# A state-space scan and a window-attention block on one core: the first image's convolution phase reordered, and the planner's PSUM banks written into the program

## The chip, the core and the metric

One core of one Trainium2 chip runs the whole program. Its engines are named as the profile names them: PE (matrix products; PEld is its weight load), DVE (vector), ACT (activation), POOL and SP (which here only issues DMAs). The metric is device microseconds (us) of one execution. Before the change three executions gave 7610.15, 7621.01 and 7637.82 us, a median of 7621.01 us.

## What is computed

The input is 8 images of 192 channels of 64x64 points, float32. Two layers follow each other. Per image:

```python
# layer 0: state-space scan
x = W_in @ x                                  # 192 -> 384 channels
x = depthwise_conv3x3(x) + b_dw               # 'SAME'
p = W_xd @ x                                  # 384 -> 16
Gl, Gm, Gr, L, U, D = (W @ p for W in ...)    # for 4 directions x 384 channels
Gl, Gm, Gr = each / (|Gl| + |Gm| + |Gr| + 1e-7)
for step in range(8):                         # chunks of 8 columns
    h = L * xs + Gl * up(h) + Gm * h + Gr * down(h)
    y += w_m[d] * (h * U + xs * D)            # 4 directions d: x, x^T, both flipped
y = grn(layernorm(y));  x = W_out @ y         # 384 -> 192
# layer 1: 8x8 windows, 6 heads, top-16 scores per row kept
s = layernorm(x); q, k, v = W_qkv @ s
x2 = s + proj(softmax(top16(normed(q) . normed(k)) + bias) @ v)
out = x2 + fc2(gelu(fc1(layernorm(x2))))
```

## The kernel before, in words

**Two parts.** A first phase, written out by hand, loads the constants and does the projection and the convolution of image 0 alone. All the rest comes from a planner: a `Plan` object collects steps (engine, cost, function, what is read and written), simulates them in `run` (L175) and hands them out in one order, in which they are then recorded (L1688 ff.). The steps are: `scan` of image b, the `front` (projection and convolution) of image b+1 and the `windows` of image b-1, side by side.

**The first phase** (L329 to L501). `load` (L334) alternates between two DMA queues, that of SP and that of ACT, so half of the constants are issued from ACT's own stream, ahead of ACT's first work. Image 0 comes in four strips of 16 rows (`xa`, `xb`, L367 and L370). There are 12 units: 3 channel tiles `ct` by 4 strips `u`. For each unit, `projected` (L432) has PE multiply by `w_in` into a PSUM tile `pin` (L439, L442) and ACT copy it into the bordered image `full` (L443). Nine units are convolved on DVE (`convolved`, L462: nine instructions over a strip, L468 and L470) and three, those of `ct` 2 with `u` 1 to 3, on PE (`convolved_by_products`, L473: nine products per half strip with a diagonal matrix `dg` that ACT makes at L487; ACT copies the sum out at L483). `stored` (L445) has ACT lay each unit out twice (`sn` L450, `st` L454), and SP writes both to DRAM (L451, L457). The order in the stream is: project unit n, convolve unit n-1 and store it; so ACT's copy of unit n+1 stands behind its stores of unit n-1. The convolution of a strip reads one row of the next strip.

**The folding** (L503 to L576). Biases and scales are folded into weights: `w_cv` from `w_dw`, `w_g2` times `w_m`, the mean taken out of `w_out`, three bias rows with small products on PE (`bias_row`, L527), `w_f1` times its norm's scale. It works in pools of its own, `prep` and `prep_ps`, which open after the pools of the convolution are closed and take over their memory, so the first instruction waits until the last store of the convolution has landed. Its loads (L506, L531, L542) are issued by SP at that place. The folded bias rows are written into their weights by a DMA from SP (L544).

**The start of the scan.** `x0`, the first chunk of image 0 (L762), goes into memory that the first phase used; then a product (L769), a copy (L779), a way through DRAM (L784, L792) and the gate products (L809) lead to the first DVE instruction of the scan (L842).

**PSUM banks.** From the scan on, six of the eight banks belong to the pool `l_ps`, all under one tag, "lp"; tiles are called `lp` or `g` (the scan's). The planner models the six banks as slots and gives a new tile the slot whose last user ended first in its simulation (L285). The recorded program does not know that slot: the tile pool gives the bank that was released first, in the order of the recorded instructions, by the last reader in that order. A tile's first product waits until the previous tile of its bank has been read for the last time; PE takes its instructions in the recorded order, so everything behind waits too.

Of the kernel before, what the change touches and what calls it, by code (L numbers as in the profile page):

```python
# [23 lines left out]
F32 = mybir.dt.float32  # L24
U8 = mybir.dt.uint8
AF = mybir.ActivationFunctionType
ALU = mybir.AluOpType
AX = mybir.AxisListType
PSUM = bass.MemoryType.PSUM
DRAM = bass.MemoryType.DRAM  # L30

P = 128
B, DM, H, W = 8, 192, 64, 64
DIN, ND, NS = 384, 4, 16
CT = DIN // P
CH = 8
HEADS, HD, WS = 6, 32, 8
HALF = DM // 2
# [6 lines left out]
RG = 32  # L45
# [9 lines left out]
class Held:  # L55


    def __init__(self, pool, shape, name, bufs=None, tag=None, dtype=F32):
        self.args = pool, shape, dtype, name, tag or name, bufs or pool.bufs
        self.tag, self.bufs = (id(pool), tag or name), bufs or pool.bufs  # L60
        self.users, self.left, self.end, self.next, self.tile = [], 0, 0.0, None, None

    def make(self):
        if self.tile is not None:
            return
        pool, shape, dtype, name, tag, bufs = self.args
        self.tile = pool.tile(shape, dtype, name=name, tag=tag, bufs=bufs)

    def __call__(self):
# [10 lines left out]
class Plan:  # L80
# [67 lines left out]
    def order(self):  # L148

        before = [s.before for s in self.steps]
        tiles = {h: h.left for s in self.steps for h in s.held}
        best = None
        for n in range(self.RUNS):
            for s, k in zip(self.steps, before):
                s.before, s.ready = k, 0.0  # L160
            for h, k in tiles.items():
                h.left, h.end, h.next = k, 0.0, None
            run = self.run()
            if best is None or self.length < best[0]:
                best = self.length, run, [s.start for s in run]
            for s in run:
                needs = [d.start for d in s.after] + [h.next.start for h in s.held if h.next]
                rank = min(needs, default=s.end) - (s.end - s.start)
                s.rank = (s.rank + rank) / 2 if n else rank
        self.length, run, starts = best  # L170
        for s, t in zip(run, starts):
            s.start = t
        return run

    def run(self):  # L175

        slots, queues = {}, {}
        counted, full = {}, {}
        done = []
# [16 lines left out]
        for s in self.steps:  # L196
            for h in s.makes:
                queues.setdefault((h.tag, s.lane), []).append(s)
                slots.setdefault(h.tag, [(0.0, k, None) for k in range(h.bufs)])
        first = {k: 0 for k in queues}  # L200

        def kept(tag):
# [58 lines left out]
        while todo:  # L261
            for e in dirty_plain:
                best_plain[e] = picked(e, None, plain[e], ready)
            for e in dirty | dirty_plain:
                best[e] = picked(e, best_plain[e], makers[e], room)
            dirty_plain, dirty = set(), set()
            e = min((x for x in engines if best[x]), key=lambda x: best[x][1])
            _, t, s = best[e]
            s.start = t
            if e == "PE":  # L270
                lead, cycles, share = s.cost
                end = stream(t + lead, cycles, share)
                free[e], s.end = end, end + 140.0
            else:
                hold, more = s.cost
                free[e] = t + hold
                s.end = free[e] + more
            (makers if s.makes else plain)[e].remove(s)
            dirty_plain.add(e)
            todo -= 1  # L280
            done.append(s)
            for tag in needs.get(s, ()):
                first[tag, s.lane] += needs[s][tag]
            for h in s.makes:
                slot = min(slots[h.tag], key=lambda x: x[:2])  # L285
                slots[h.tag].remove(slot)
                if slot[2]:
                    slot[2].next = s
            touched = bool(s.makes)
            for h in s.held:  # L290
                h.left -= 1
                h.end = max(h.end, s.end)
                if not h.left:
                    slots[h.tag].append((h.end + self.HOP, h.users[0].n + h.bufs, h))
                    touched = True
            for d in s.after:
                d.before -= 1
                d.ready = max(d.ready, s.end + (self.HOP if d.engine != e else 30.0))
                if not d.before:
                    wake(d)  # L300
                    if not d.makes:
                        dirty_plain.add(d.engine)
                    elif d.lane:
                        dirty.add(d.engine)
                    else:
                        touched = True
            if touched:
                dirty.update(engines)
# [10 lines left out]
def tile_ss2d_then_window_attention(ctx: ExitStack, tc: tile.TileContext, a: dict, out: bass.AP):  # L319
# [6 lines left out]
    nc = tc.nc  # L326
# [1 line left out]

    const = ctx.enter_context(tc.tile_pool(name="const", bufs=1))  # L329

    queues = [nc.sync, nc.scalar]
    n_loads = 0

    def load(name, src=None, rows=None):  # L334

        nonlocal n_loads
        src = a[name] if src is None else src
        shape = list(src.shape)
        t = const.tile([rows or shape[0]] + shape[1:], F32, tag=name, name=name)
        if rows:  # L340
            nc.gpsimd.memset(t[HALF:rows], 0.0)
        queues[n_loads % 2].dma_start(t[0 : shape[0]], src)
        n_loads += 1
        return t

    def blank(name, shape, value=None, engine=nc.gpsimd):
# [12 lines left out]
    ident = blank("ident", [P, P])  # L359
    make_identity(nc, ident)  # L360

    w_in = load("w_in")
    w_dv = load("w_dv")
    xa = epool.tile([P, H, W], F32, name="xa")
    xb = epool.tile([P, NG // 2, 8, W], F32, name="xb")
    for u in range(NG // 2):
        nc.sync.dma_start(xa[:, 16 * u : 16 * u + 16, :], x[0, 0:P, 16 * u : 16 * u + 16, :])  # L367
        for k in range(2):
            row = 16 * u + 8 * k
            nc.scalar.dma_start(xb[64 * k : 64 * k + 64, u], x[0, P:DM, row : row + 8, :])  # L370
        if u == 0:
            vecs = load("vecs")
    full = [epool.tile([P, H + 2, W + 2], F32, name=f"full{ct}") for ct in range(CT)]
    for t in full:
        nc.vector.memset(t[:, 0 : H + 2 : H + 1, :], 0.0)
# [50 lines left out]
        h.make()  # L426
    with early, tc.tile_pool(name="early_ps", bufs=2, space=PSUM) as early_ps:

        taps = [(dy, dx) for dy in range(3) for dx in range(3)]
        dg = epool.tile([P, 9, P], F32, name="dg")  # L430

# [30 lines left out]
        def convolved(ct, u):  # L462

            acc = epool.tile([P, 16, W], F32, name="acc", bufs=3)
            for n, tap in enumerate(taps):
                w = w_dv[:, ct, n : n + 1]
                if n == 0:
                    nc.vector.tensor_scalar(acc, near(ct, u, *tap), w, b_dw[:, ct : ct + 1], ALU.mult, ALU.add)  # L468
                else:
                    nc.vector.scalar_tensor_tensor(acc, near(ct, u, *tap), w, acc, ALU.mult, ALU.add)  # L470
            stored(ct, u, acc)

        def convolved_by_products(ct, u):  # L473

            acc = epool.tile([P, 16, W], F32, name="acc", bufs=3)
            for k in range(2):
                pc = early_ps.tile([P, CH, W], F32, name="pc")
                for n, (dy, dx) in enumerate(taps):
# [4 lines left out]
                nc.scalar.activation(acc[:, 8 * k : 8 * k + 8, :], pc, AF.Identity, bias=b_dw[:, ct : ct + 1])  # L483
            stored(ct, u, acc)

        for n in range(9):
            nc.scalar.activation(dg[:, n, :], ident, AF.Copy, scale=w_dv[:, CT - 1, n : n + 1])  # L487
        units = [(ct, u) for ct in range(CT) for u in range(NG // 2)]
        by_vector = [(ct, u) for ct, u in units if ct < CT - 1 or u == 0]
        by_tensor = [c for c in units if c not in by_vector]  # L490
        done = 0
        for ct, u in units:
            projected(ct, u)
            while done < len(by_vector) and by_vector[done] < (ct, u):
                convolved(*by_vector[done])
                done += 1
            while by_tensor and by_tensor[0] < (ct, u):
                convolved_by_products(*by_tensor.pop(0))
        for c in by_tensor:
            convolved_by_products(*c)  # L500
        assert done == len(by_vector)  # L501

    with tc.tile_pool(name="prep", bufs=2) as prep, tc.tile_pool(name="prep_ps", bufs=2, space=PSUM) as prep_ps:  # L503

        w_dw = prep.tile([3 * RG, CT * 4 * 3], F32, name="w_dw")
        nc.sync.dma_start(w_dw, a["w_dw"])  # L506
        id3 = prep.tile([3 * RG, RG], F32, name="id3")
        nc.vector.tensor_add(id3, ident[0 : 3 * RG, 0:RG], ident[0 : 3 * RG, RG : 2 * RG])
        nc.vector.tensor_add(id3, id3, ident[0 : 3 * RG, 2 * RG : 3 * RG])
# [17 lines left out]
        def bias_row(name, dst, products, *more):  # L527

            n = dst.shape[-1]
            row = prep.tile([1, n], F32, name="row_" + name)  # L530
            nc.sync.dma_start(row, a[name])  # L531
            for at in range(0, n, 384):
                m = min(384, n - at)
                ps = prep_ps.tile([P, 512], F32, name="ps_pre")
# [3 lines left out]
                    )  # L538
                nc.vector.tensor_add(row[:, at : at + m], row[:, at : at + m], ps[0:1, 0:m])
            for extra in more:  # L540
                got = prep.tile([1, n], F32, name="more_" + name)
                nc.sync.dma_start(got, a[extra])  # L542
                nc.vector.tensor_add(row, row, got)
            nc.sync.dma_start(dst[HALF : HALF + 1, 1, :], row)  # L544


        bias_row("b_qk", w_qk, [(n1_b[:, ci : ci + 1], w_qk[0:HALF, ci, :]) for ci in range(2)])
# [1225 lines left out]
```

## Time and profile before

| what | us |
|---|---|
| three runs, median | 7621.01 |
| the profiled execution, its own time | 7623.82 |
| its span, first to last instruction | 7622.0 |
| PE busy (share of the span) | 6699.8 (88%) |
| DVE busy | 6364.3 (83%) |
| POOL busy | 6229.7 (82%) |
| ACT busy | 4896.1 (64%) |
| mean granted PE clock (share of full) | 0.860 |

Busy time is per engine and overlaps. Idle time stands in the rows in front of the instruction that ended it, with the releaser: who set the semaphore it waited for last. In a timeline a row merges like instructions: start, busy us, engine, line, operation, how many; in square brackets the idle time before. ACTq and SPq are the parts of ACT and SP that issue DMAs. The end of a matrix product is modelled in the trace, so PE's busy time is not PE at its peak.

### The profile page before, as it was taken

What the parts mean: (1) busy time and instruction counts of PE and PEld (TensorE: products, weight loads), DVE (VectorE), ACT (ScalarE), POOL (GpSimd) and SP (SyncE); (2) the same over time, 40 slices, a digit from 0 to 9 for tenths busy, and PEclk for the clock granted to TensorE, in tenths of its full rate; (3) what the DMA queues carried; (4) which work ended last, traced back from release to release, by engine and by line L of the source; (5) the groups of instructions that cost most, each with busy time, mean ns of one, the idle gap of its engine ahead of it and who ended that gap; (6) DMA issues with size and microseconds to landing.
All of it is one profiled execution on the core that took longest, in us unless ns stands there. A gap on an engine that the chain in (4) does not pass through costs nothing. (4 is left out here: it accounts for less than half of the span.)

```text
span 7622.0 us, 141764 instructions
## 1 busy us (share of the span) xinstructions
PE 6699.8 (88%) x50180; PEld 3458.4 (45%) x50180; DVE 6364.3 (83%) x15477; ACT 4896.1 (64%) x9649; POOL 6229.7 (82%) x6333
## 2 busy tenths in 40 slices
PE   5888789988998899888999899988888888888987
PEld 2333344444444444444444444444444444444554
DVE  5687788998899988988888988889899989889643
ACT  2455456765776657675777757766576756666665
POOL 0688888998899988988888888889899989899422
PEclk7888789987988889898998889988888878888999
DMA  3666455312551245312551135411211111111100
GB/s 107 164 174 163 121 139 135 101 51 75 154 145 46 55 134 151 89 46 78 157 139 47 50 105 143 124 50 46 60 50 50 49 59 52 49 45 45 32 22 14
DMA packets 988331, 669.39 MB, mean 88 GB/s; under 512 B 651972, under 2 KB 814215, under 8 KB 987623
## 3 DMA queue, kind: packets, MB, share of 16 engines
q1 hardware_dynamic: 985638, 656.86, 32.1%
q8 instruction: 398, 6.52, 0.4%
q10 hardware_dynamic: 1984, 3.48, 0.2%
q14 instruction: 311, 2.54, 0.1%
HBM read 433.98 MB, written 226.18 MB: 87 GB/s over the span
## 5 line engine op out<-in xcount | busy, mean ns | idle before, releaser
L809 PE MATMUL g<-xe,w_g 32*128 32x512 f32 x3648 | 1171.5, 749 | 224.4 <-DVE dx L968 74.6
L809 PE MATMUL g<-xo,w_g 32*128 32x512 f32 x3648 | 1189.1, 729 | 184.5 <-DVE dx L968 90.9
L866 ACT ACTIVATE ab<-g 128x512 f32<-128x512 f32 x1344 | 784.6, 596 | 393.0 <-PE nb L809 168.9
L897 POOL TENSOR_TENSOR ab<-ab 128x512 f32<-128x512 f32 x672 | 865.0, 1287 | 162.7 <-ACT ab L866 151.0
L929 POOL TENSOR_TENSOR pw<-pw,rr 128x512 f32<-128x512 f32 x672 | 867.4, 1291 | 135.6 <-ACT rr L912 115.4
L914 POOL TENSOR_TENSOR pw<-pw,pq 128x512 f32<-128x512 f32 x672 | 881.0, 1311 | 82.5 <-DVE pq L873 53.2
L918 POOL TENSOR_TENSOR pw<-pw,pq 128x512 f32<-128x512 f32 x672 | 878.1, 1307 | 15.5
L982 POOL TENSOR_TENSOR dx<-dx,hu 128x512 f32<-128x512 f32 x576 | 742.9, 1298 | 112.1 <-DVE hu L973 97.1
L910 ACT ACTIVATE rr<-nb,eps 128x512 f32<-128x512 f32 x672 | 462.0, 687 | 571.7 <-DVE nb L907 569.1
L809 PEld LDWEIGHTS g<-xo,w_g 32*128 32x128 f32 x3648 | 410.5, 208 | 719.3 <-DVE dx L968 192.9
L809 PEld LDWEIGHTS g<-xe,w_g 32*128 32x128 f32 x3648 | 408.9, 212 | 704.8 <-DVE dx L968 173.1
L1628 PE MATMUL lp<-hd,w_f 128*64 128x256 f32 (+1 forms) x2304 | 594.9, 497 | 56.1 <-ACT hd L1614 15.0
L990 POOL TENSOR_TENSOR y<-y,dx 128x512 f32<-128x512 f32 x384 | 597.6, 1563 | 2.2
L696 PE MATMUL lp<-strip,w_cv 128*32 128x256 f32 x8064 | 563.5, 418 | 27.6 <-DMA strip<-pad 19.2
L925 DVE SCALAR_TENSOR_TENSOR nb<-nb,rr 128x512 f32<-128x512 f32 x672 | 464.8, 692 | 142.5 <-ACT rr L912 140.3
L934 DVE SCALAR_TENSOR_TENSOR nb<-nb,pw 128x512 f32<-128x512 f32 x672 | 464.7, 692 | 138.4 <-POOL pw L929 136.2
L907 DVE TENSOR_TENSOR nb<-nb,ab 128x512 f32<-128x512 f32 x672 | 465.3, 692 | 113.1 <-POOL ab L897 103.5
L973 DVE TENSOR_TENSOR hu<-g,hid 128x512 f32<-128x512 f32 x768 | 518.7, 681 | 1.0 <-PE g L809 0.7
L809 PE MATMUL nb<-xe,w_g 32*128 32x512 f32 x672 | 479.1, 800 | 12.5 <-DVE hid L942 12.3
L888 ACT ACTIVATE nb<-nb 128x512 f32<-128x512 f32 x672 | 399.5, 594 | 137.7 <-DVE pq L875 78.2
L980 POOL TENSOR_TENSOR y<-hu,dx 128x512 f32<-128x512 f32 x192 | 246.3, 1289 | 291.7 <-DVE hu L973 289.7
L809 PE MATMUL nb<-xo,w_g 32*128 32x512 f32 x672 | 463.1, 774 | 14.6 <-DVE hid L942 14.6
(221 smaller groups left out, 16684.8 us busy)
## 6 DMA issues: line engine op xcount, KB each, us to landing
strip<-pad SPq DMA_DIRECT2D x1008, 132.0 KB
xd<-xsT SPq DMA_DIRECT2D x384, 256.0 KB
x<-xs SPq DMA_DIRECT2D x64, 768.0 KB
xd<-xs SPq DMA_DIRECT2D x192, 256.0 KB
z<-y SPq DMA_DIRECT2D x64, 768.0 KB
zg<-z SPq DMA_DIRECT2D x64, 768.0 KB
pad<-xin SPq DMA_DIRECT2D x168, 264.0 KB
xsT<-sn SPq DMA_DIRECT2D x168, 256.0 KB
```

Of the source, the lines that this page charges most:

```text
L696: nc.tensor.matmul(pc()[q * RG : (q + 1) * RG, k * 256 : (k + 1) * 256].rearrange("p (h w) -> p h w", h=4), lhsT=w_cv[:, ct, q, dx, :], rh ...
L809: nc.tensor.matmul(dst, lhsT=w[rows, col : col + P], rhs=xp[rows, :], start=True, stop=True)
L866: lambda r=r: nc.scalar.activation(ab()[:, r, :], g[r](), AF.Abs),
L897: plan("POOL", gp(512), lambda: nc.gpsimd.tensor_add(ab()[:, 0, :], ab()[:, 0, :], ab()[:, 1, :]), w=[ab])
L907: plan("DVE", vec(512), lambda: nc.vector.tensor_add(nb(), nb(), ab()[:, 0, :]), r=[ab], w=[nb])
L914: plan("POOL", gp(512), lambda: nc.gpsimd.tensor_add(one(), one(), pq()[:, 0, :]), r=[(pq, 0)], w=[pw])
L918: lambda: nc.gpsimd.tensor_add(one(), one(), pq()[:, 1, :]),
L929: plan("POOL", gp(512), lambda: nc.gpsimd.tensor_mul(one(), one(), rr()), r=[rr], w=[pw])
L973: lambda: nc.vector.tensor_mul(like(hu(), d), like(pu(), d), state(d, ct)),
L982: plan("POOL", gp(512), lambda: nc.gpsimd.tensor_add(dx(), dx(), hu()), r=[hu], w=[dx])
L990: nc.gpsimd.tensor_add(y, y, dx().rearrange("p (c i) -> p i c", c=CH))
L1628: nc.tensor.matmul(dst[:, at : at + rhs.shape[-1]], lhsT=lhsT, rhs=rhs, **flags)
```

## The change

Two independent things.

**First phase.** All constants but `w_in`, `w_dv` and `vecs` are issued by SP. All 12 units are projected first, in one run; `dg` is made after the fourth. Then the nine DVE units follow in order, each with its store, and after the fifth, seventh and eighth of them one unit by products each, whose `acc_p` has two buffers of its own. The `prep` pool is opened together with the convolution's pools instead of behind them, its loads are issued before the convolution, and the folding uses the convolution's PSUM pool. The folded bias rows are written into the weights from ACT's queue instead of SP's.

**Banks.** The planner remembers the number of the slot that it gave each tile, and keeps those of its best run. When a tile under "lp" is made, it asks for the tag of its slot, "lp0" to "lp5", with one buffer each: so it gets the planned bank.

```diff
 class Held:
+        self.slot = 0
     def make(self):
         pool, shape, dtype, name, tag, bufs = self.args
+        if tag == "lp":
+            tag, bufs = f"{tag}{self.slot}", 1
         self.tile = pool.tile(shape, dtype, name=name, tag=tag, bufs=bufs)
...
-                best = self.length, run, [s.start for s in run]
+                best = self.length, run, [s.start for s in run], {h: h.slot for h in tiles}
...
-        self.length, run, starts = best
+        self.length, run, starts, slots = best
+        for h, k in slots.items():
+            h.slot = k
...
                 slot = min(slots[h.tag], key=lambda x: x[:2])
                 slots[h.tag].remove(slot)
+                h.slot = slot[3]
...
-    queues = [nc.sync, nc.scalar]
-    def load(name, src=None, rows=None):
+    def load(name, src=None, rows=None, queue=nc.sync):
...
-        queues[n_loads % 2].dma_start(t[0 : shape[0]], src)
-        n_loads += 1
+        queue.dma_start(t[0 : shape[0]], src)
...
-    w_in = load("w_in")
-    w_dv = load("w_dv")
+    w_in = load("w_in", queue=nc.scalar)
+    w_dv = load("w_dv", queue=nc.scalar)
...
-            vecs = load("vecs")
+            vecs = load("vecs", queue=nc.scalar)
...
+        prep = early.enter_context(tc.tile_pool(name="prep", bufs=1))
+        w_dw = prep.tile([3 * RG, CT * 4 * 3], F32, name="w_dw")
+        nc.sync.dma_start(w_dw, a["w_dw"])
+        added = {}
+        for name in ("b_qk", "b_pr", "n1_br"):
+            added[name] = prep.tile([1, a[name].shape[-1]], F32, name="row_" + name)
+            nc.sync.dma_start(added[name], a[name])
...
-            acc = epool.tile([P, 16, W], F32, name="acc", bufs=3)
+            acc = epool.tile([P, 16, W], F32, name="acc_p", bufs=2)
...
-        for n in range(9):
-            nc.scalar.activation(dg[:, n, :], ident, AF.Copy, scale=w_dv[:, CT - 1, n : n + 1])
...
-        for ct, u in units:
+        for n, (ct, u) in enumerate(units):
             projected(ct, u)
-            while done < len(by_vector) and by_vector[done] < (ct, u):
-                convolved(*by_vector[done])
-                done += 1
-            while by_tensor and by_tensor[0] < (ct, u):
-                convolved_by_products(*by_tensor.pop(0))
-        for c in by_tensor:
-            convolved_by_products(*c)
+            if n == 3:
+                for m in range(9):
+                    nc.scalar.activation(dg[:, m, :], ident, AF.Copy, scale=w_dv[:, CT - 1, m : m + 1])
+        for n, c in enumerate(by_vector):
+            acc = convolved(*c)
+            stored(*c, acc)
+            if n in (4, 6, 7):
+                convolved_by_products(CT - 1, (4, 6, 7).index(n) + 1)
 
-    with tc.tile_pool(name="prep", bufs=2) as prep, tc.tile_pool(name="prep_ps", bufs=2, space=PSUM) as prep_ps:
-
-        w_dw = prep.tile([3 * RG, CT * 4 * 3], F32, name="w_dw")
-        nc.sync.dma_start(w_dw, a["w_dw"])
+        prep_ps = early_ps
...
-            nc.sync.dma_start(dst[HALF : HALF + 1, 1, :], row)
+            nc.scalar.dma_start(dst[HALF : HALF + 1, 1, :], row)
```

## The prediction

> **What bounds the kernel now.** I read four views: the slices, the table of engines by stage, the timeline of the first 230 us, and the waits of PE. The slices first:
>
> ```profile
> PE   5888789988998899888999899988888888888987
> DVE  5687788998899988988888988889899989889643
> POOL 0688888998899988988888888889899989899422
> ```
>
> From the third slice (190 us each) to the last three, PE, DVE and POOL are all at eight or nine tenths: no engine is the bound alone, and a stall of one is soon a stall of the others. The first slice is another regime: POOL at zero, PE and DVE half busy. Only there can much be won by order. The timeline of DVE (start, busy us, engine, line, operation, count, idle before) shows its skeleton:
>
> ```profile
> 27.42 0.81 DVE L468 TENSOR_SCALAR acc<-full,w_dv,vecs 128x1024 f32<-128x1024 f32 x1 [25.28 <-ACT full L443]
> ...
> 118.99 10.60 DVE L470 SCALAR_TENSOR_TENSOR acc<-full,w_dv,acc 128x1024 f32<-128x1024 f32 x8
> 181.33 0.19 DVE L508 TENSOR_TENSOR id<-ident 96x32 f32<-96x32 f32 x1 [51.74 <-DMA xs<-st]
> ...
> 183.10 1.35 DVE L510 TENSOR_TENSOR w_cv<-id,w_dw 96x1152 f32<-96x1152 f32 x1 [1.36 <-DMA w_dw<-in_w_dw_dram]
> ...
> 200.09 0.36 DVE L576 TENSOR_TENSOR rpb<-rpb,top_b 128x192 f32<-128x192 f32 x1
> 223.14 0.69 DVE L842 TENSOR_TENSOR hid<-g,x 128x512 f32<-128x512 f32 x1 [22.70 <-PE g L809]
> ```
>
> Nine convolved units run from 27.42 to 129.6 without a gap (11.35 each); then DVE stands still for 51.74 us, because the three units by products run after it on PE (products 122.15 to 174.0) and the folding's memory is free only when the last store has landed; then the folding, 181.33 to 200.45; then 22.70 us until the scan. SP issues the load of `x0` at 200.47, at the end of DVE's last folding instruction. So the whole phase is one chain, and all three big engines wait for its end. Why it starts late is in ACT's rows:
>
> ```profile
> 19.68 2.75 ACTq L342 DMA_DIRECT2D w_f<-in_w_f_dram  x2
> 22.46 1.28 ACT L487 ACT_TABLE_LOAD   x1 [22.46 <-DMA temp<-in_temp_dram]
> 23.75 2.74 ACT L487 ACTIVATE dg<-ident,w_dv 128x128 f32<-128x128 f32 x9
> 26.39 1.91 ACT L443 COPY full<-pin 128x1024 f32<-128x1024 f32 x2
> ```
>
> PE had the first `pin` at 11.62 (10.28 + 1.34, L442); ACT copied it at 26.39, behind its DMA issues, its table and `dg`.
>
> **The first phase, step by step.** The times are those of the new order, made of rows of the old one.
>
> 1. *Start.* ACT now issues 11 DMAs ahead of its first work: eight `xb` (7.63), `w_dv` (0.41) and two that SP issued before at 0.40 and 0.43. From 0.71 that is until 9.6; with the table (1.28) 10.9. `pin` is there at 11.6, the copy takes 1.05: DVE begins at about 12.8 instead of 27.42. `dg` (2.74) goes behind the fourth copy, where PE has a second `pin` to fill. The loads go to SP, whose stream ended at 27.76: eleven more there, 12 us by ACT's rows without `xb`'s, make 40, and SP's next work, the first store, is due near 48. Loads later than that would cost nothing until the stores' three buffers are full.
>
> 2. *Nine units on DVE.* 9 x 11.35 = 102.2, as before, if `acc` is free. It has three buffers, and ACT now copies all 12 projections before it stores the first unit. Unit 4 begins at 12.8 + 3 x 11.35 = 46.9 if unit 1 has been stored. PE's later units in each burst take 1.98 + 1.13 = 3.11 (rows at 32.23 and 34.15): 11.6 + 11 x 3.11 = 45.8 for the last product, +1.05 copy, +1.05 and +1.98 for the first store = 49.8. So DVE stalls 2.9 and ends at 12.8 + 102.2 + 2.9 = 117.9. This is where the new order is nearest to a loss; the clock decides:
>
> ```profile
> 40.00:60.00 20.00, 10.93 (x16) 3.36 (x16) 19.36 (x16) 6.47 (x7) 0.00 (x0) 0.62 0.38 105
> 140.00:160.00 20.00, 20.00 (x49) 8.53 (x48) 0.00 (x0) 6.48 (x8) 0.00 (x0) 1.00 0.19 52
> ```
>
> (busy PE, PEld, DVE, ACT, POOL; then the granted clock.) In the old order PE works in bursts and gets 0.62; busy throughout it gets 1.00. At 27.44, after 12.8 idle, four products take 3.78, a few us later 1.98. The new projections are one run, so I take the fast row. The Trainium skill ("TensorE: Matmul & The Clock Gate", Part 1: The HAM clock gate) says it as a rule: half speed by default, full after some 3.4 us of sustained work, and half again after an idle window. Against it, the same page warns that the gate was seen stuck low; by that the sum would be the cold rival's below.
>
> 3. *Three units by products.* 15.5 each warm (31.17 for two). The first two half strips can run from 46; the rest follow as ACT frees `pc` behind the stores of units 5, 7 and 8: the last is summed near 115, copied and laid out (2 x 0.69 + 1.05 + 1.98) by 119.5. The last DVE unit is stored by 122, issued by SP at 122; before, the last issue at 177.70 let DVE go at 181.33, 3.6 later, so 126. All of it lies beside DVE; the cover is the folding, to 135, 9 us.
>
> 4. *Folding.* 181.33 to 200.45 = 19.1 before. Two waits for its loads go (1.36, and 0.52 for `more_b_pr`): 17.2. The 51.74 go wholly: no memory is waited for. What is late next is the folding's own chain, PE and DVE in turn (13.51 and 4.95 of mutual waits are in the 17.2). 117.9 + 17.2 = 135.1. The two bias stores (0.65, 0.53) move to ACT's stream, idle until PE's first planned product behind the folding; without that cover 1.2. SP loses them ahead of `xt`; `x0` waits for the folding, not for SP.
>
> 5. *Onward.* `x0` at 135.1 instead of 200.47: **65 us**. The 22.7 to the scan are the same instructions. Behind it, the recorded order of every engine is the same as before, instruction for instruction, so the rest moves as a block, but for the banks.
>
> **The banks.** I followed each of the 6360 tiles of the six banks through the instruction records, with its predecessor in the bank by each program's order. 5428 keep theirs, 932 get another. In the old trace 580 tiles wait for their bank, 539 us of PE's 910 idle; but only 74 of these are among the 932, with 69 us. Put the new predecessor's end, in the same trace, in place of the old: 37.8 us of PE's idle go (67 tiles), 11.2 come (42 tiles, held back where they were not). The commonest wait of PE (us in total, times, longest), and the clearest single case:
>
> ```profile
> PE g L809 <- DVE dx L968: 165.5, 110, 7.1
> ```
>
> ```profile
> 3905.30 1.05 PE L1453 MATMUL lp<-ident,at 128*128 128x128 f32 x4 [4.27 <-DVE hu L973]
> ```
>
> The first is a bank wait: `dx` and `hu` are the last readers of a `g`. In the second, PE stands 4.27 us for a `hu` while the bank of the new plan had been free 3.6 us earlier. Net 26.6 on PE. How much of it reaches the end no row says: all of it if PE never waits for another engine, nothing if it always would have. PE is the busiest at 88%, with DVE and POOL at 83 and 82, so I take half, **13**; the ends kept are 38 gained and 11 lost.
>
> **Sum.** 7623.8 (profiled execution, 1.8 around the span, 2.8 over the median) - 65 - 13 = **7546**. The first phase may be 58 to 68 (stall 0 to 10), the banks +11 to -38: 7518 to 7577. 0.3%, about 23 us, is what a measurement can tell from no change.
>
> **Rivals.**
>
> *Cold projections.* If PE gets the clock of the old bursts: 3.78 + 1.3 a unit, last product at 6.6 + 12 x 5.1 = 67.8, first store done at 71.9 instead of 49.8. DVE stalls 25 instead of 2.9, the phase gains 43: **7568**. For it: 0.62 in the row of the old phase. Against: 1.00 where PE is busy throughout. 0.10.
>
> *The planned banks let out a cascade.* Each wait that goes brings the next products closer to the plan, and others of the 539 us, on tiles whose bank is the same, shrink too. A tenth of them beyond the forecast is 54: **7492**. For it: the engines are locked together. Against: these waits have the same predecessor. 0.07.
>
> *The phase's gain is spent in the scan of image 0.* The slices show that second stage at eight tenths, and `strip` loads there wait for DMA; if the front, not `x0`, led it, SP's stream would still start it, from 122 instead of 194, so little could be lost. Half of 65: **7578**. 0.04.
>
> *Slower: the planned banks are freed later than planned.* 462 of the 932 tiles get a predecessor that ended later in the old trace, by 315 us together. The planner's ends are a model's; the old order asked only who was read first. All 315 on PE: 7624 - 65 + 315 = 7874. It decides from 65 + 23 = 88, more than a quarter of the 315; the trace shows 11.2, 4%, the rest being covered by products in front. **7700**, say, at 45%. 0.03.
>
> *It doesn't do what it says.* The recorded orders show that it does: ACT's copies ahead of the stores, 932 other banks. Only the effect could be nil, if ACT were held by something else to 26: then step 1 is lost (14.6) and the stall too: **7558**, inside the range. 0.02, with the forecast at 0.74.
>
> **How the numbers follow.** Forecast 7518 to 7577 with 0.74. To leave out no more than 0.2 with the uncertain share of the banks, the range goes up over the cold case and part way to the cascade: **7505 to 7595**. Faster by over 0.3%: 0.74 + 0.10 + 0.07 + 0.04 + 0.02, less 0.03 for milder ends of the slower case that eat up the gain: 0.94. Within: 0.03. Slower: 0.03.
>
> **What would show it.** Step 1: DVE's first L477 near 12.8. Step 2: no idle over 10 us between the units, PE's projections in one run at 3.1 each. Step 4: no wait for a store ahead of the folding; `x0` issued near 135, the scan's first DVE instruction near 158. Banks: PE's idle, 910 us, down by about 90: 65 of the first phase's, the rest from bank waits; the row of `dx` at L809 smaller. I am wrong if the first scan instruction comes after 175, or if it comes at 158 and the span is still not near 7545: then the banks, or the block that I moved unchanged, are it.

## The result and the profile after

The changed kernel takes **7548.4 us** (median of four runs, 7541.67 to 7558.15); the kernel before, four runs beside it, 7626.0 (7610.15 to 7637.82). The ratio is 0.9896, 95% interval [0.9878, 0.9913]. The forecast was 7546 in a range of 7505 to 7595. The profiled execution took 7551.0 us, its span is 7549.2 (before 7622.0).

The slices of the changed kernel, now 189 us each:

```profile
PE   7888799898989899888999899989888888898887
DVE  6787798988899889898898988889899988899543
POOL 1898788998899989987988888889899989899422
```

Only the first slice is another one: PE seven tenths instead of five, POOL already begins in it. From the second on, the rows look as they did. The timeline of DVE (start, busy, engine, line, operation, count, idle before) has a new skeleton:

```profile
14.64 0.83 DVE L477 TENSOR_SCALAR acc<-full,w_dv,vecs 128x1024 f32<-128x1024 f32 x1 [12.50 <-DMA xb<-in_x_dram]
...
48.74 0.81 DVE L477 TENSOR_SCALAR acc<-full,w_dv,vecs 128x1024 f32<-128x1024 f32 x1
...
106.02 10.53 DVE L479 SCALAR_TENSOR_TENSOR acc<-full,w_dv,acc 128x1024 f32<-128x1024 f32 x8
116.47 0.18 DVE L510 TENSOR_TENSOR id<-ident 96x32 f32<-96x32 f32 x1
...
132.45 0.16 DVE L568 TENSOR_TENSOR b_f<-b_f,ps_pre 128x6 f32<-128x6 f32 x1 [5.44 <-PE ps_pre L565]
...
133.96 0.36 DVE L575 TENSOR_TENSOR rpb<-rpb,top_b 128x192 f32<-128x192 f32 x1
153.72 0.69 DVE L841 TENSOR_TENSOR hid<-g,x 128x512 f32<-128x512 f32 x1 [19.40 <-PE g L808]
```

The first unit begins at 14.64 (before 27.42). The fourth, 48.74, has no idle before it. The folding begins as the ninth unit ends, 116.47, where 51.74 us of waiting stood. The scan starts at 153.72 instead of 223.14: **69.4 us earlier**. The same DVE instructions later run 65.9 us earlier around 300 us, 73.3 around 3000, 65.9 around 5000, and 72.8 at the end. So the first phase brings nearly all of it.

PE in the same execution: the twelve projections end at 44.65, then the products of the three units, then the folding's and the front's.

```profile
44.65 15.72 PE L489 MATMUL pc<-full,dg 128*128 128x512 f32 x36
74.93 17.19 PE L489 MATMUL pc<-full,dg 128*128 128x512 f32 x36 [14.56 <-ACT acc_p L492]
97.47 17.87 PE L489 MATMUL pc<-full,dg 128*128 128x512 f32 x36 [5.35 <-ACT acc_p L492]
...
126.18 6.23 PE L565 MATMUL ps_pre<-n_gb,w_f 128*128 128x1 f32 x24
132.71 3.56 PE L649 MATMUL lp<-xt,w_in 128*128 128x512 f32 x4 [0.30 <-issue]
136.21 1.13 PE L652 MATMUL lp<-xt,w_in 64*128 64x512 f32 x4
137.27 0.86 PE L768 MATMUL lp<-x,w_xd 128*32 128x128 f32 x24
```

And SP's issues:

```profile
121.70 0.36 SPq L466 DMA_DIRECT2D xs<-st  x1
...
126.66 0.59 SPq L761 DMA_DIRECT2D x<-xs  x1
```

`x0` (L761) is issued at 126.66, 8 us ahead of the folding's end. Its product (L768) still starts only at 137.27: PE takes it behind L565, L649 and L652. The scan now waits for PE's queue, not for `x0`.

PE's commonest wait, which was to shrink:

```profile
PE g L808 <- DVE dx L967: 176.1, 110, 7.1
```

The wait of `g` for `dx` is 176.1 us, where it was 165.5.

### The profile page after: what moved, and what is told of

It is laid out like the page before. It is cut to its first block, busy times and chain, and to the rows that moved or that the text cites. A ratio compares the mean times of both kernels' runs of the same rounds, so it can differ in the third digit from the quotient of the medians.

```text
span 7549.2 us, 141750 instructions
## 1 busy us (share of the span) xinstructions
PE 6680.5 (88%) x50180; PEld 3448.8 (46%) x50180; DVE 6360.6 (84%) x15477; ACT 4895.1 (65%) x9649; POOL 6227.8 (82%) x6333
## 3 DMA queue, kind: packets, MB, share of 16 engines
q8 instruction: 398, 6.52, 0.4%
## 5 line engine op out<-in xcount | busy, mean ns | idle before, releaser
L695 PE MATMUL lp<-strip,w_cv 128*32 128x256 f32 x8064 | 566.8, 420 | 27.3 <-DMA strip<-pad 22.7
L941 DVE TENSOR_TENSOR hid<-lx,nb 128x512 f32<-128x512 f32 x672 | 454.2, 676 | 4.9
```

The lines of the kernel that those rows point to most:

```text
L695: nc.tensor.matmul(pc()[q * RG : (q + 1) * RG, k * 256 : (k + 1) * 256].rearrange("p (h w) -> p h w", h=4), lhsT=w_cv[:, ct, q, dx, :], rh ...
```

## The experiments

Each kernel differs from the changed one, unless another base is named. There are twelve runs, four on each of three chips, each four beside the kernel before on the same chip (medians 7624.32, 7632.32 and 7636.99).

### The two halves by themselves

**Phase alone:** the tiles go back to the one tag.

```diff
-        if tag == "lp":
-            tag, bufs = f"{tag}{self.slot}", 1
```

> The new first phase with the pool choosing the banks as before. Theory A (both parts gain, the phase nearly all of it: the offset between the two traces is 65.9 us at 300 us and 72.8 at the end): the scan's first DVE instruction at 153.7 us as in the changed kernel, and 60 to 67 us below the kernel before, so 5 to 9 us above the changed one; PE's waits for banks near 539 us again. Theory B (the banks are worth the 13 us that I forecast, or more): 13 or more above the changed one, 60 or less below the kernel before. Theory C (the banks do nothing, the difference between the offsets is chance): within 3 us of the changed one.

Measured 7562.37 (7553.37 to 7565.91), ratio 0.9916 [0.9902, 0.9929], 62 below before. The scan starts at 153.10, as in the changed kernel.

**Banks alone:** the kernel before, with the planner's slots and the tags `lp0` to `lp5`.

```diff
+        if tag == "lp":
+            tag, bufs = f"{tag}{self.slot}", 1
...
+                h.slot = slot[3]
```

> The first phase as before, the planned banks. Theory A: 5 to 9 us below the kernel before, the scan's first DVE instruction at 223.1 us. Theory B: 13 us or more below. Theory C: within 3 us of it. The rival that banks freed late cost time: above it.

Measured 7616.76 (7609.95 to 7628.35, eleven runs), ratio 0.9989 [0.998, 0.9998]: 8 below before, 2 to 15 by the interval.

**Both once more, on one chip**, since 7548.4 and 7562.37 were not measured beside each other:

> The changed kernel once more, on the same chip as the next three, so that differences of ten microseconds need not be taken across chips. Both theories: 7535 to 7560 us; it is the base of the differences below.

> The phase alone (no planned banks), beside the changed kernel on one chip. Theory A (the banks are worth what they were worth alone, some 8 us): 5 to 11 us above the changed kernel. Theory B (half of PE's net bank waits reaches the end, as predicted): 13 us or more above it. Theory C (the banks are worth nothing behind the new phase): within 3 us of it.

The changed kernel: 7546.12 (7542.41 to 7547.88), ratio 0.9881 [0.9868, 0.9895]. The phase alone: 7566.28 (7560.0 to 7572.85), ratio 0.9907 [0.9894, 0.9921]. The ranges don't touch: behind the new phase the banks are worth 20 us here, 14 by the two medians before, and not the 8 that they are worth alone. Theory B holds in its size; the next section shows that its reason doesn't. The phase by itself is worth 62 and 71.

Where do the 14 to 20 us stand? PE's row in the engine tables of the phase alone (both profiles), then of the changed kernel's second profile (the first has PE 6680.5):

```profile
PE 6707.2 (89%) x50180; PEld 3460.8 (46%) x50180; DVE 6368.6 (84%) x15477; ACT 4894.1 (65%) x9649; POOL 6228.0 (82%) x6333
```

```profile
PE 6710.7 (89%) x50180; PEld 3459.3 (46%) x50180; DVE 6362.2 (84%) x15477; ACT 4892.5 (65%) x9649; POOL 6222.6 (82%) x6333
```

```profile
PE 6675.6 (89%) x50180; PEld 3444.9 (46%) x50180; DVE 6360.3 (84%) x15477; ACT 4893.5 (65%) x9649; POOL 6228.4 (83%) x6333
```

The spans are 7564.1, 7571.0 and 7540.6. PE's idle, that is span less busy PE, is 856.9 and 860.3 for the phase alone, 868.7 and 865.0 with the banks: PE does *not* wait less. It is busy for 27 to 35 us less, and the granted clock is 0.861 in both profiles of the phase alone, 0.864 and 0.865 with the banks. In these four profiles the fall has the size of the clock's difference: 6709 x 0.861 / 0.8645 = 6682. But both profiles of the phase alone are of its slowest execution at its lowest clock, and the clock of every execution is on record. On the one chip, three executions of the phase alone at 0.865, 0.866 and 0.867 took 7566.28, 7570.14 and 7560.0; the four of the changed kernel at 0.864 to 0.866 took 7542.41 to 7547.88. At equal clocks the 20 us are still there, so the clock does not explain them. In these profiles, whose spans lie 23 us apart in the mean, the difference arises late: at 3000 us the phase alone ran 71.4 and 68.5 us ahead of before (its two profiles), at the end 57.9 and 51.0; the changed kernel 73.3 and 78.0, at the end 72.8 and 81.4. Alone, the banks did it otherwise: PE's idle 922 to 904, its busy time 6699.8 to 6712.4, the clock 0.860 in both.

### Do waits for banks reach the end at all?

Each tile gets, of the banks that are free in the plan, the one freed **last** instead of first. 5021 tiles get another predecessor than in the changed kernel; nothing else changes.

```diff
+        free = [0.0] * 6
+        for s in run:
+            for h in s.makes:
+                if h.args[4] == "lp":
+                    h.slot = max((k for k in range(6) if free[k] <= s.start + 1e-3), key=lambda k: free[k])
+                    free[h.slot] = h.end + self.HOP
```

> The changed kernel with the same order of instructions, but each tile takes the free bank that by the plan was freed last instead of first. 5021 of 6360 tiles get another predecessor. In the trace of the changed kernel, the new predecessors end later than the tile's first product began by 1720 us in sum, and 208 us of waits would go; each wait delays all behind it, so that most of the sum overlaps. Theory A (waits for banks reach the end in part): PE's waits for banks up by some hundreds of us and the span up by about half of that, 100 to 600 us. The rival (PE's waits are covered by DVE and POOL): the span up by under 50 us. It measures what share of a wait for a bank arrives at the end.

Measured 7570.11 (two runs, 7568.08 and 7572.15), ratio 0.9928 [0.991, 0.9946]; its span is 7566.3. Its row of the engine table, and the row of `dx`:

```profile
PE 5934.5 (78%) x50180; PEld 3029.2 (40%) x50180; DVE 6374.8 (84%) x15477; ACT 4886.4 (65%) x9649; POOL 6228.9 (82%) x6333
```

```profile
PE g L814 <- DVE dx L973: 382.4, 207, 7.6
```

PE's idle, span less busy, is 1631.8 us where it was 868.7 in the changed kernel, and the waits for `dx` went from 176.1 to 382.4. So 763 us more waiting cost some 22 us by the medians (17 between the spans, 24 by the ratios), about 3%; the two kernels were not measured beside each other, and on its own chip this one is 8 above the phase alone. The rival of the expectation held. Where the rest went is in the groups of the scan's gate products, first of the changed kernel, then of this one (busy us, mean ns of one, idle before):

```profile
L808 PE MATMUL g<-xe,w_g 32*128 32x512 f32 x3648 | 1165.2, 749 | 228.5 <-DVE dx L967 80.5
L808 PE MATMUL g<-xo,w_g 32*128 32x512 f32 x3648 | 1201.7, 730 | 186.3 <-DVE dx L967 95.6
```

```profile
L814 PE MATMUL g<-xo,w_g 32*128 32x512 f32 x3648 | 796.9, 757 | 541.8 <-DVE dx L973 185.1
L814 PE MATMUL g<-xe,w_g 32*128 32x512 f32 x3648 | 806.9, 775 | 509.1 <-DVE dx L973 197.3
```

As many products, each as long or a little longer, but busy for 1604 us instead of 2367: a product uses 32 rows, and those that are held back are then seen running beside each other. In these two groups the idle grew by 636 us and the busy time fell by 763. PE at 88% was no bound: at 78% the program takes nearly the same time.

### One part of the first phase at a time

**Projections between the units again** (unit n projected, then n-1 convolved; the loads, `acc_p` and the folding stay as changed).

```diff
-        for n, c in enumerate(by_vector):
-            acc = convolved(*c)
-            stored(*c, acc)
-            if n in (4, 6, 7):
-                convolved_by_products(CT - 1, (4, 6, 7).index(n) + 1)
+            for c in units[n - 1 : n]:
+                if c in by_vector:
+                    stored(*c, convolved(*c))
+                else:
+                    convolved_by_products(*c)
+        convolved_by_products(*units[-1])
```

> The changed kernel with one part of the phase undone: projection n, then unit n-1, as before; the folding's pool and loads early, SP's loads and the banks as changed. Theory A (projecting all first is what lets PE's three units run beside DVE's nine): DVE's units still end near 117, but PE's last unit ends near 161 and the folding's products stand behind it; the scan begins near 194 us, 41 us later than in the changed kernel, and the span is 35 to 45 us above it. Rival (the folding's early pool alone brings the gain): under 10 us above it.

Measured 7586.72 (7580.17 to 7595.43), ratio 0.9937 [0.9922, 0.9952]. DVE's units end at 117.19, near the changed kernel's 116.3, but the products come last on PE, until 161.6:

```profile
163.09 0.54 DVE L541 TENSOR_TENSOR row_b_qk<-row_b_qk,ps_pre 1x384 f32<-1x384 f32 x1 [38.79 <-PE ps_pre L538]
...
191.22 0.69 DVE L842 TENSOR_TENSOR hid<-g,x 128x512 f32<-128x512 f32 x1 [20.65 <-PE g L809]
```

Opening the pools early helps only in part when the folding's own products (L538) stand behind the convolution's on PE: a wait of 38.79 us stands where 51.74 stood, under another name.

**Folding behind the convolution again** (its pools and its four loads).

```diff
-        prep_ps = early_ps
+    with tc.tile_pool(name="prep", bufs=1) as prep, tc.tile_pool(name="prep_ps", bufs=2, space=PSUM) as prep_ps:
+        w_dw = prep.tile([3 * RG, CT * 4 * 3], F32, name="w_dw")
+        nc.sync.dma_start(w_dw, a["w_dw"])
...
```

> The changed kernel with the folding in pools of its own again, opened behind the convolution's, its four loads there, the rest as changed. Theory A: the folding waits until the last store has landed, near 125.5, 9 us after DVE's last unit, and 1 to 3 us for its loads; the scan begins 10 to 15 us later than in the changed kernel and the span is 8 to 15 us above it. Rival (the old wait of 51.74 us was the pool's): 30 us or more above it.

Measured 7564.15 (7558.94 to 7565.58), ratio 0.9906 [0.9891, 0.9921].

```profile
127.04 0.19 DVE L510 TENSOR_TENSOR id<-ident 96x32 f32<-96x32 f32 x1 [10.03 <-DMA xs<-st]
129.32 1.35 DVE L512 TENSOR_TENSOR w_cv<-id,w_dw 96x1152 f32<-96x1152 f32 x1 [1.87 <-DMA w_dw<-in_w_dw_dram]
...
168.44 0.69 DVE L841 TENSOR_TENSOR hid<-g,x 128x512 f32<-128x512 f32 x1 [21.77 <-PE g L808]
```

The wait for the last store returns with 10.03, that for the load with 1.87.

**Nine loads back on ACT's stream** (`w_xd`, `w_g2`, `w_out`, `w_v`, `w_pr`, `n1_b`, `temp`, `w_f1`, `w_f2`).

```diff
-    w_xd = load("w_xd")
+    w_xd = load("w_xd", queue=nc.scalar)
...
```

> The changed kernel with nine of the constants' loads (w_xd, w_g2, w_out, w_v, w_pr, n1_b, temp, w_f1, w_f2) issued from ACT again. Theory A (ACT's issue of loads holds back its first copy): ACT's first copy at 23.5 to 25 instead of 13.6, DVE's first unit 10 to 11 us later, the scan and the span 9 to 13 us later. Rival (the loads' order on SP matters, not ACT's stream): within 4 us of the changed kernel.

Measured 7557.64 (7551.26 to 7560.62), ratio 0.9897 [0.9883, 0.9912]: by the ratio no different from the changed kernel's 0.9896, by the medians 9 more, on another chip. So once more beside it:

> Nine loads back on ACT's stream, beside the changed kernel on one chip. Theory A (the 14.3 us by which the scan starts later reach the end, but for the 4 to 5 that the profile showed given back): 8 to 13 us above the changed kernel. Theory B (the earlier start of DVE is covered by what follows): within 4 us of it.

Measured 7561.3 (7555.06 to 7568.48), ratio 0.9902 [0.9889, 0.9916], 15 above the changed kernel's 7546.12, whose range it doesn't touch. Theory B falls, and A's bound of 13 is passed a little: the whole delay arrives. In the first of the two profiles ACT copies its first `pin` at 26.20:

```profile
24.90 1.28 ACT L452 ACT_TABLE_LOAD   x1 [24.90 <-DMA b_f<-in_b_f_dram]
26.20 1.93 ACT L452 COPY full<-pin 128x1024 f32<-128x1024 f32 x2
```

```profile
27.25 0.82 DVE L477 TENSOR_SCALAR acc<-full,w_dv,vecs 128x1024 f32<-128x1024 f32 x1 [25.11 <-ACT full L452]
...
63.70 0.81 DVE L477 TENSOR_SCALAR acc<-full,w_dv,vecs 128x1024 f32<-128x1024 f32 x1 [2.29 <-ACT st L463]
```

### Going on: what is next on the chain

**Eight units on DVE, four by products.** In the changed kernel PE idles 14.56 and 5.35 us between its units.

```diff
-        by_vector = [(ct, u) for ct, u in units if ct < CT - 1 or u == 0]
+        by_vector = [(ct, u) for ct, u in units if ct < CT - 1]
...
-            if n in (4, 6, 7):
-                convolved_by_products(CT - 1, (4, 6, 7).index(n) + 1)
+            if n in (2, 4, 5, 6):
+                convolved_by_products(CT - 1, (2, 4, 5, 6).index(n))
```

> The changed kernel with one more unit convolved by products on PE and one fewer on DVE: eight and four. Theory (DVE's chain of units sets the end of the phase, PE has 20 us idle between its three units): DVE's units end 11.3 us earlier, at 105; PE's fourth unit ends near 107; the folding's first instruction at 105, the scan 8 to 11 us earlier, and so the span. The rival: PE's products, in order ahead of the folding's, set the end now: under 5 us earlier.

Measured 7535.85 (7534.9 to 7541.4), ratio 0.9884 [0.9871, 0.9898]. PE does the four in one run, beside DVE's eight units, which end at 105.67:

```profile
44.84 62.07 PE L489 MATMUL pc<-full,dg 128*128 128x512 f32 x144
106.85 1.45 PE L537 MATMUL ps_pre<-w_qk,n_b 96*1 96x384 f32 x4
```

**And `b_f1`'s products ahead of the other bias products**, so that DVE doesn't wait 5.44 for L565. The block moves up; its addition and scaling stand ahead of the `b_qk` row.

```diff
+        ps = prep_ps.tile([P, 512], F32, name="ps_pre")
+        for m in range(NM):
...
+        nc.vector.tensor_add(b_f1, b_f1, ps[:, 0:NM])
...
         bias_row("b_qk", ...)
```

> Eight units on DVE and four on PE, and the folding's 24 small products for b_f1 (6.23 us on PE, for which DVE waited 5.44) ahead of the other products of the folding instead of behind them. Theory (the end of the phase is a chain through PE's in-order products, not through DVE): PE is done with the folding 5 to 6 us earlier than with eight and four alone, the first planned product, the scan and the span too: 5 us below that kernel, 14 to 17 us below the changed one. Rival (x0's load or the front's loads set the scan's start now): no better than eight and four alone.

Measured 7533.73 (7530.04 to 7535.97), ratio 0.9866 [0.9849, 0.9882]. The scan starts at 139.77, 2.3 earlier than without, not 5. PE is through with the folding at 116.56 and now stands for SP's next loads:

```profile
119.57 3.75 PE L650 MATMUL lp<-xt,w_in 128*128 128x512 f32 x4 [3.01 <-DMA xt<-in_x_dram]
```

Beside the changed kernel on one chip:

> Eight units on DVE, four by products, and b_f1's products ahead of the folding's others, beside the changed kernel on one chip. Theory A (every microsecond by which the scan starts earlier reaches the end): the scan starts 13.9 earlier, so 12 to 17 us below the changed kernel. Theory B (the rest of the program takes back what the first phase gives, as it does for some 3 us in the changed kernel): 6 or less below it.

Measured 7530.24 (7526.56 to 7532.87), ratio 0.9861 [0.9847, 0.9874]: 16 below the changed kernel, and the fastest version of all.

Put together, the start of the scan against the end, both against the changed kernel:

| version | scan starts | median |
|---|---|---|
| projections between | +37.5 | +38 |
| folding behind | +14.7 | +16 |
| loads on ACT (same chip) | +14.6 | +15 |
| eight and four | -11.6 | -13 |
| and products first (same chip) | -13.5 | -16 |

Over 50 us, a microsecond of the first phase is about a microsecond of the program. The other three rows compare kernels that were not measured beside each other: by the ratios to the kernel before, their last column would be +31, +8 and -9, and two profiles of the changed kernel differ by 8.6 in their spans. But four of the versions ran on one chip. Against the last of them (products first, scan at 139.77), projections between has its scan 51.5 later and its median 53.0 higher, folding behind 28.7 and 30.4, loads on ACT 28.2 and 23.9.

## Why the prediction held, and where it did not

**Sum.** 7546 against 7548.4. It stood on two terms, 65 and 13, together 78; against the kernel before beside it the changed kernel gained 77.6, and on another chip 90.9 (7636.99 to 7546.12). That the sum hit to within 2.4 us is partly luck: the parts measured 62 to 71 and 8 to 20, and the second did not come the way that I thought.

**Step 1, start** (12.8; measured 14.64). ACT's issues end at 12.27, not 9.6. The timeline of ACT has the gap:

```profile
1.65 1.26 ACTq L371 DMA_DIRECT2D xb<-in_x_dram  x2
2.94 0.73 ACTq L344 DMA_DIRECT2D vecs<-in_vecs_dram  x1
6.52 5.75 ACTq L371 DMA_DIRECT2D xb<-in_x_dram  x6
12.30 1.28 ACT L452 ACT_TABLE_LOAD   x1 [12.30 <-DMA xb<-in_x_dram]
13.59 1.02 ACT L452 COPY full<-pin 128x1024 f32<-128x1024 f32 x1
```

Between 3.67 and 6.52 ACT issues nothing, though the next load waits for no data: I added up issue times and left out that a stream of loads can stand. The remedy itself was rightly named: with nine loads back on ACT the first unit begins 12.3 later (27.31 against 15.02 on one chip) and the program ends 15 later. The Trainium skill ("DMA: Bandwidth & Descriptors", section "Issuing engines are not separate DMA queues") holds that issuing from several engines saves only the sequencer's time, usually small beside the DMA; here that time was ACT's own, ahead of its first copy, and these 12.3 us are what it costs: the nine issues themselves take 4.9 of them, the rest is mostly gaps in which the stream stood.

**Step 2, nine units** (stall 2.9, end 117.9; measured no stall, 116.5). The projections ran warm and in one run, as predicted, but 2.97 a unit instead of 3.11 (L448 and L451 overlap), and the store of the first unit ended 0.09 us ahead of the fourth's start: 48.65 against 48.74. The later start and the missing stall nearly cancel. With the loads on ACT the stall did appear, 1.27 and 2.29. The cold rival fell: over 20 to 40 us, with the projections alone on PE, the clock was 1.00, and so it was over 40 to 60, where it had been 0.62.

```profile
20.00:40.00 20.00, 20.00 (x55) 6.66 (x54) 19.36 (x17) 9.62 (x16) 0.00 (x0) 1.00 0.47 117
40.00:60.00 20.00, 20.00 (x50) 8.00 (x48) 19.43 (x16) 10.43 (x11) 0.00 (x0) 1.00 0.57 158
```

(busy PE, PEld, DVE, ACT, POOL, then the clock.)

**Step 3, products** (last store 122; measured 121.70). They lay beside DVE and the folding covered the last store. Moving the folding back shows the cover's size: 10.03.

**Step 4, folding** (17.2; measured 116.47 to 134.32 = 17.85). The two waits for loads went; the one for L565 grew from 4.95 to 5.44.

**Step 5, onward** (`x0` at 135.1, scan near 158; measured 126.66 and 153.72). Wrong in its reason: I took `x0`'s memory to be that of the last folding instructions, and it was not. Before, SP waited ahead of this issue for the last of them (`rpb`, 3.7 us); now it waits 0.7 us for the landing of the last store to `xs`, which `x0` reads. `x0` came 8.4 earlier, the scan only 4.3, since PE was busy with L565 until 132.4 and then with the front's first product. From the folding's end to the scan it was 19.40 instead of 22.7. So the phase is worth more than the 65 at the scan's start: 69.4 here, and 68.3 to 70.0 in the other profiles with this whole phase. In this profile 3.5 of it were gone again by 300 us; in the second profile of the same kernel nothing was (69.8 at the scan's start, 71.4 at 300 us), so that loss is no property of the change. By the medians the phase alone is worth 62 and 71.

**The banks** (13; measured 8 alone, 14 and 20 behind the new phase). The size was in the bounds, the path was not. The step that failed is "so I take half": it took PE at 88% as the nearest to a bound and let half of its waits reach the end. The version with 763 us more waiting on PE lost some 22, about 3%; at that price 26.6 fewer would be worth under one. The sign "the row of `dx` smaller" did not come: 165.5 became 176.1. PE's idle, span less busy, fell by 53.5 where 90 was predicted, and with the banks it is 5 to 12 us more than with the phase alone. The single case that I quoted, 4.27 for `hu`, did go: no wait for `hu` is left at that line. So the gain does not come by shorter waits of PE, as I had it, and it is there at equal clocks too. The Trainium skill ("TensorE: Matmul & The Clock Gate", "A second HAM failure mode: psum-queue depth-cycling") tells of small idles between products, with PSUM banks cycled through, that make the clock fall back. The direction agrees with the profiles' 0.861 and 0.865 here, but not with the other executions, in which the clocks are equal and the difference stays; no run shows that this is the cause. It **stays open** why the planned banks gain more behind the new phase.

**The rivals.** "Slower: banks freed later than planned" priced waits in full and at 45%; the late banks add 763 us to PE's idle, where the whole of it before was 922, and end some 22 us later, so its 315 would hardly have decided. The cascade (7492) did not come. "Spent in the scan of image 0" came to 3.5 of 69.4 in one profile and to nothing in the other.

## What to carry to other kernels

Where a serial phase stands ahead of a balanced one, follow the chain to the first instruction of the next stage and move whole engines' work under the longest; among the versions compared on one chip, what the scan's start moved arrived at the end to within 5 us, over 13 to 51 us. Read two queues for each thing you move: the one it leaves, and the one in which its successor stands, for the wait returns there under another name (38.79 for PE's products, 3.01 for SP's loads). Do not price a wait on a shared engine by that engine's busy share: here 763 us more idle of the busiest engine cost some 22. Nor does that price tell what another choice of banks brings: the planned ones gained 8 to 20.

## What the runs showed of the hardware

- Products on 32 rows that are released together are recorded as running side by side: 7296 of them took 2367 us of PE when spread, 1604 when held back and bunched, with means of 730 to 749 and 757 to 775 ns. So busy PE depends on how its work is spaced, and can fall by 746 us without a gain.
- The same 24 tiny products of L565 take 6.23 us shortly after PE has idled 6.93, at a granted clock of 0.50; directly behind the convolution's products (L513 of products first) they take 3.88, at 0.94. The same work costs more or less by its place on PE.
